# Exponentials handed to ScalarE's DMA queue, and three written-out orders, in a kernel of 64 graphs with two layers of graph attention

## The chip, the cores and the metric

The kernel runs on one core of a Trainium2 chip, in float32. The metric is the device time of one execution in microseconds (us). A core has TensorE (PE; its weight loads are PEld), VectorE (DVE), ScalarE (ACT), GpSimd (POOL) and SyncE (SP); engines run their own instruction streams in order and wait for one another by semaphores. DMAs are issued by an engine's queue and carried out by 16 DMA engines.

## The reference, cut to what matters

There are 64 graphs of 256 nodes with 512 features. Each passes through two layers; the first holds two attention stages (four heads of 256, then one head of 512), the second one stage (eight heads of 64). Weights are shared by all graphs.

```python
def gat_layer(x, mask, W, a_src, a_dst, bias, concat):
    xl = (x @ W).reshape(B, N, H, F)
    e = leaky_relu(asrc[:, :, None, :] + adst[:, None, :, :], 0.2)   # asrc, adst: xl . a_src, xl . a_dst
    attn = softmax(where(mask[..., None], e, NEG_INF), axis=1)
    out = einsum('bsdh,bshf->bdhf', attn, xl)
    return out + bias
# layer 0
h = maximum(layernorm(x), 0)
mask = (adj > 0) | eye(N)
x = x + gat_layer(elu(gat_layer(h, mask, W1, ...)), mask, W2, ...)
# layer 1
h = maximum(layernorm(x), 0)
xp = h @ W_proj                              # 8 heads of 64
scores = leaky_relu(a_src_i + a_dst_j + b_att, 0.2), -1e30 where adj is 0
x = x + relu(softmax(scores, axis=-1) @ xp)
```

## The kernel before

A graph is taken as two tiles of 128 nodes. Each large product (m1a and m1b for the two halves of W1, m2 for W2, m3 for W_proj) is a `Product`: seven smaller products p1 to p7 in place of eight, of sums and differences of operand blocks. Its matmuls are at L54; ACT copies the partial sums that are still needed (`kept`, L60); `put` adds and writes the results (`total`, L251 on ACT, L253 on DVE). TensorE's results go to three pools of PSUM banks: `ps_mm` (4 banks), `ps_sum` (2) and `ps_tr` (2).

The exponential of leaky_relu(a + o) is the larger of two products of exponentials, so only vectors go through the exponential function. `exp1`, `exp2` and `exp3` compute three vectors each on ACT (L275, and L461 to L465 for the third stage), and `spread` lays one of them out along the free axis on all partitions: a small DMA writes it to DRAM (`kept`, L240), further ones read it back as `bc` rows (L245; two heads each). Both are issued by SP. Then `edges1`, `edges2`, `edges3` call `weigh` once per tile: ACT writes `wy` (L280, three buffers), DVE writes the weights `e` (L281, nine buffers), masked by `mask` (L299, L301) or by `cap`, which `caps` makes on ACT (L308 to L312) and `cap3` transposes by two DMAs of SP (L363).

The steps of a graph are, in order of data: `load` (SP), `stats1` and `norm1` (L170 to L178, ACT's L195), `away1` (two DMAs of SP through DRAM that rearrange blocks of 32 for the transpose, L207 and L208), `turn1` (DVE's 32 x 32 transposes L213, then POOL's sums L219 to L222; graph 0 has `turn0`, L342 and L343, in their place), m1a and m1b, `exp1`, `edges1`, `gat1` (L382), `out1` (DVE L390 and L392, then ACT's two `ez`, L395 and L396), `elu1` (L401), `turn2` (TensorE L201, ACT L410), m2, `exp2`, `edges2`, `gat2` (L433), `out2` (L440, L443), `stats3`, `norm3`, `turn3` (L201, L233), m3, `exp3`, `edges3`, `gat3` (L482), `out3` (L488, L490, POOL's L492), `range` (L495, L496; the ranges of the exponentials), and `store` (SP, L499, 512 KB from `x2`). POOL's `bias` (L352) adds the second stage's bias to the input. A second, general program follows the loop; it starts only if a range is extreme.

For `norm1` ACT writes its output in a mixed order of columns, so that the block that DVE's L213 reads after the two DMAs is contiguous.

The program text sets each engine's order. One string, `order`, lists the steps of a round with an offset for the graph; the loop over r from -1 to 66 runs it for each round and leaves out steps of graphs that don't exist. So up to four graphs are in work at once, and the first and last graphs follow the same order with holes in it. The products of graph 0's m1b and its 32 dots (`dot`, DVE: attention vectors folded into W1's columns) are written ahead of the loop; further dots for W2, W_proj's products and sums (POOL's L593, DVE's L595) and the differences of weight blocks (`right`, L518), come from two generators, one piece after each step.

Of the kernel before, what the change touches and what calls it, by code (L numbers as in the profile page):

```python
# [17 lines left out]
P = 128  # L18
# [79 lines left out]
def short_path(ctx, tc, flags, x, adj, w1, att_src1, att_dst1, b1, w2, att_src2, att_dst2, b2, w_proj, w_att,  # L98
# [84 lines left out]


    def mixed(h):
        return h.rearrange("p (a c i) -> p a c i", a=4, c=4)

    def unmixed(x):
        return x.rearrange("p (a i c) -> p a c i", a=4, c=4)

    def norm(src, rstd, off, mix):
        h = work.tile([P, T, D], F32, name="h", bufs=1)
        for t in range(T):
            to, of = (mixed(h[:, t]), unmixed(src[:, t])) if mix else (h[:, t, :], src[:, t, :])
            nc.scalar.activation(to, of, AF.Relu, bias=off[:, t:t + 1], scale=rstd[:, t:t + 1])  # L195
        return h
# [6 lines left out]
    def away(h):  # L203


        kept = dram.tile([T, 4, P, P], F32, name="kept_h")
        nc.sync.dma_start(kept.rearrange("t a p e -> p t a e"), h.rearrange("p t (a e) -> p t a e", a=4))  # L207
        nc.sync.dma_start(h, kept.rearrange("t a (j q) e -> (a j) t (q e)", q=4))  # L208

    def back(h, a):  # L210

        for t in range(T):
            nc.vector.transpose(a[:, 4 * t:4 * t + 2].rearrange("p r k (j q) -> p q (r k) j", q=4),  # L213
                                h[:, t].rearrange("p (q c i) -> p q c i", q=4, c=4))
# [22 lines left out]
    def spread(w, heads):  # L237

        kept = dram.tile([heads, P, T], F32, name=f"kept{heads}")
        nc.sync.dma_start(kept.rearrange("h p t -> p h t"), w)  # L240
# [6 lines left out]
        return rows  # L247

# [34 lines left out]
    class Graph:  # L283
# [41 lines left out]
        def norm1(self):  # L325
            self.h = norm(self.xs, *self.ro, True)
# [88 lines left out]
        def exp2(self):  # L415
            exps(lambda sl: self.ex2[:, sl].rearrange("p h t -> p t h"), 1, xl2[:, :, 0, :L2], xl2[:, :, 1, :L2])
            self.bc2 = spread(self.ex2[:, 2:3], 1)

        def edges2(self):
            e = self.e[2] = work.tile([P, T, N], F32, name="e", bufs=9)  # L420
            for s in range(T):
                weigh(e[:, s, :], self.bc2[0], self.ex2[:, 0, s:s + 1], self.ex2[:, 1, s:s + 1],
# [31 lines left out]
        def norm3(self):  # L454
            self.h = norm(self.x2, *self.ro, False)
# [4 lines left out]
        def exp3(self):  # L460
# [6 lines left out]
            self.bc3 = spread(self.ex3[:, 2], H3)  # L467

        def edges3(self, h):
            e = self.e[3, h] = work.tile([P, T, N], F32, name="e", bufs=9)  # L470
            for s in range(T):
                weigh(e[:, s, :], self.bc3[h], self.ex3[:, 0, h, s:s + 1], self.ex3[:, 1, h, s:s + 1],
# [54 lines left out]
    va2 = small.tile([P, HC, 2, 2], F32, name="va2", bufs=1)  # L527
    graphs[0].load()
# [8 lines left out]
    graphs[0].turn0()  # L537
# [10 lines left out]
    def column(r, s, h, c):  # L548
        dot(blocks(w1_sb[0])[r][s][:, c, h:h + 1], blocks(w1_sb[h // 2])[r][h % 2][:, c, -Q:], att1[s][:, h, :])


    dots = [(r, s, h, c) for i in range(2) for s in range(2) for r in range(2) for h in (2 - 2 * i, 3 - 2 * i)
            for c in range(2)]
    first = [d for d in dots if d[0] == 0 and d[2] == 3]
    for d in first:
        dots.remove(d)
        column(*d)
    for _ in right(w1_sb[1]):
        pass
    m1b = graphs[0].m1[1]  # L560
    for part in (m1b.p1, m1b.p2, m1b.p5, m1b.p6, m1b.p7, m1b.c22, m1b.p4, m1b.p3):
        part()
        for d in dots[:4]:
            column(*d)
        del dots[:4]
    for _ in right(w1_sb[0]):
        pass

    def weights_for_0():
        for r in range(2):  # L570
            for c in range(4):
                for s in range(2):
                    for half in range(2):
                        dot(va2[:, 4 * r + c, s, half:half + 1], blocks(w2_sb)[r][half][:, c, -Q:],
                            att2[s][:, half * Q:(half + 1) * Q])
                    yield
        for r in range(2):
            for s in range(2):
                v = va2[:, 4 * r:4 * r + 4, s]
# [331 lines left out]
```

## Time and profile before

| what | value |
|---|---|
| median of 3 runs | 3298.52 us (3297.95 to 3301.16) |
| profiled execution, its own time | 3308.74 us |
| its span, first to last instruction | 3307.0 us |
| mean granted TensorE clock | 0.988 |
| busy share of PE, DVE, ACT, POOL | 95%, 68%, 61%, 35% |
| DMA traffic | 280.36 MB, mean 85 GB/s |

A busy share is the time in which an engine executes, as a share of the span. A group of instructions is one line of the kernel on one engine: its busy time and the mean duration of one, then the idle time of the engine just ahead of them, and what ended most of it. In a timeline the columns are start, duration, engine, line, operation, operands and count; the wait ahead of it stands in brackets, with what ended it. In a row of windows the first figures are the stretch and its length, then busy time (and instructions) of PE, PEld, DVE, ACT and POOL, then the granted clock, the DMA share and GB/s.

### The profile page before, as it was taken

Reading aid. Unit: us, or ns where it says so; the run is one execution under the profiler, and the core shown is the slowest. Engines: PE = TensorE matmul, PEld = TensorE weight load, DVE = VectorE, ACT = ScalarE, POOL = GpSimd, SP = SyncE. Lnnn points to the kernel's source line nnn. Section 1 sums busy time; section 2 is a strip of 40 time slices with the busy share of each in tenths; the row PEclk is TensorE's granted clock in tenths of the full one; section 3 lists DMA queues with packets and bytes.
Section 4 is the critical chain, followed back from the end, with each engine's and each line's share of the span. In section 5 each row is a group of like instructions: output and inputs, shape, how many; then the busy total and the mean of one; then the engine's idle time right before and its main releaser. Section 6 shows DMA issues by size and latency. Waiting matters only on the chain. (4 is left out here: it accounts for less than half of the span.)

```text
span 3307.0 us, 60191 instructions
## 1 busy us (share of the span) xinstructions
PE 3153.8 (95%) x21772; PEld 2657.8 (80%) x21772; DVE 2237.4 (68%) x6189; ACT 2031.4 (61%) x4867; POOL 1172.9 (35%) x1433
## 2 busy tenths in 40 slices
PE   4999999999999999999999999999999999999996
PEld 3788888888888888888888878888888888888885
DVE  7567667667667666676676676676676676766764
ACT  2566666666666666666666665666666666666663
POOL 2343343342332333433433433433423323334332
PEclk7999999999999999999999999999999999999998
DMA  4232332323333333323223333223233333232231
GB/s 132 61 87 78 93 87 78 93 78 87 86 82 90 85 82 90 79 82 92 82 84 93 81 78 93 87 78 91 78 89 86 82 90 85 81 92 81 80 87 48
DMA packets 352653, 280.36 MB, mean 85 GB/s; under 512 B 159200, under 2 KB 253408, under 8 KB 352352
## 3 DMA queue, kind: packets, MB, share of 16 engines
q1 hardware_dynamic: 350976, 274.35, 30.4%
q8 instruction: 176, 2.88, 0.4%
q10 hardware_dynamic: 1376, 2.10, 0.2%
q14 instruction: 125, 1.02, 0.2%
HBM read 200.54 MB, written 67.44 MB: 81 GB/s over the span
## 5 line engine op out<-in xcount | busy, mean ns | idle before, releaser
L280 ACT ACTIVATE wy<-bc,exs 128x256 f32<-128x256 f32 x1664 | 761.7, 524 | 328.6 <-DMA bc<-kept 276.7
L382 PE MATMUL pm<-xl,e 128*128 128x257 f32 x2048 | 504.9, 390 | 95.2 <-DVE e L281 45.0
L253 DVE TENSOR_TENSOR xl<-pm,kept 128x256 f32<-128x256 f32 (+2 forms) x768 | 321.1, 418 | 360.0 <-PE pm L54 285.8
L60 ACT ACTIVATE kept<-sum 128x264 f32<-128x264 f32 (+3 forms) x768 | 286.3, 381 | 399.3 <-PE sum L54 399.2
L281 DVE SCALAR_TENSOR_TENSOR e<-wy,exs,cap 128x256 f32<-128x256 f32 x1024 | 450.8, 481 | 110.2 <-ACT wy L280 110.2
L382 PEld LDWEIGHTS pm<-xl,e 128*128 128x128 f32 x2048 | 356.0, 190 | 207.8 <-DVE e L281 69.2
L54 PE MATMUL sum<-w_sb,h1s 128*128 128x257 f32 x2048 | 489.3, 381 | 2.7 <-ACT h1s L410 1.9
L492 POOL TENSOR_TENSOR x<-x,o 128x256 f32<-128x256 f32 x256 | 196.8, 769 | 788.2 <-DVE o L490 788.2
L54 PEld LDWEIGHTS sum<-w_sb,h1s 128*128 128x128 f32 x2048 | 389.8, 191 | 62.8 <-ACT h1s L410 2.3
L281 DVE SCALAR_TENSOR_TENSOR e<-wy,exs,mask 128x256 f32<-128x256 f32 x640 | 303.2, 527 | 111.1 <-ACT wy L280 111.1
L54 PE MATMUL pm<-w_sb,h1s 128*128 128x257 f32 x1536 | 366.9, 381 | 0.0
L178 POOL TENSOR_TENSOR rstd<-ve,neg_half 128x2 f32<-128x2 f32 x128 | 90.0, 703 | 670.2 <-DVE ve L176 663.8
L54 PEld LDWEIGHTS pm<-w_sb,h1s 128*128 128x128 f32 x1536 | 288.8, 190 | 47.4 <-ACT h1s L410 0.2
L482 PEld LDWEIGHTS pm<-xl,e 128*64 128x64 f32 x8192 | 255.3, 139 | 57.5 <-issue 30.9
L482 PE MATMUL pm<-xl,e 128*64 128x65 f32 x8192 | 274.0, 225 | 13.2 <-DVE e L281 13.0
L54 PE MATMUL sum<-w1a_sb,hs 128*128 128x260 f32 x1024 | 274.1, 390 | 4.5 <-ACT kept L60 1.7
L54 PE MATMUL sum<-wp_sb,hs 128*128 128x264 f32 x1024 | 271.0, 387 | 0.5 <-ACT kept L60 0.5
L54 PE MATMUL sum<-w1b_sb,hs 128*128 128x256 f32 x1024 | 264.0, 380 | 3.0 <-ACT hs L343 1.9
L392 DVE SCALAR_TENSOR_TENSOR z<-pm,r,b_sb 128x256 f32<-128x256 f32 x512 | 247.9, 484 | 18.3
L433 PE MATMUL pm<-xl,e 128*128 128x257 f32 (+1 forms) x1024 | 244.0, 381 | 1.8 <-DVE e L281 1.8
L395 ACT ACTIVATE ez<-z 128x512 f32<-128x512 f32 x256 | 160.1, 626 | 127.0 <-DVE z L392 127.0
L54 PEld LDWEIGHTS sum<-w1a_sb,hs 128*128 128x128 f32 x1024 | 189.7, 191 | 47.1 <-issue 13.7
(94 smaller groups left out, 4998.8 us busy)
## 6 DMA issues: line engine op xcount, KB each, us to landing
bc<-kept SPq DMA_DIRECT2D x384, 256.0 KB, 3.7
xs<-in_x_dram SPq DMA_DIRECT2D x64, 512.0 KB, 3.9
out_dram<-x SPq DMA_DIRECT2D x64, 512.0 KB, 8.5
kept_h<-h SPq DMA_DIRECT2D x63, 512.0 KB, 3.2
h<-kept_h SPq DMA_DIRECT2D x63, 512.0 KB, 3.6
ad<-in_adj_dram SPq DMA_DIRECT2D x64, 256.0 KB, 4.7
bc<-kept SPq DMA_DIRECT2D x64, 128.0 KB, 4.0
w_sb<-in_L_gnn_W_dram SPq DMA_DIRECT2D x4, 512.0 KB
```

The costliest lines, as they stand in the source:

```text
L54: self.nc.tensor.matmul(to[:, :self.n], self.lhs[:, i, c, :], self.rhs[:, i, c, :], start=(first and c == 0), stop=(last and c == self.nk ...
L60: self.nc.scalar.activation(s[:, :self.n], self.sum[:, :self.n], AF.Copy)
L178: nc.gpsimd.tensor_tensor(rstd, ve[:, 0, :], neg_half, ALU.pow)
L253: nc.vector.tensor_tensor(dst, pm, add, ALU.add)
L280: nc.scalar.activation(wy, bc, AF.Copy, scale=yw)
L281: nc.vector.scalar_tensor_tensor(dst, wy.rearrange("p t q -> p (t q)"), xw, mask, ALU.max, op)
L382: nc.tensor.matmul(pm[:, :Q + 1], self.e[1, h][:, s, t * P:(t + 1) * P], xl1[:, s, h, L1:], start=(s == 0), stop=(s == T - 1))
L392: nc.vector.scalar_tensor_tensor(z[:, sl], pm[:, :Q], r, b1_sb[:, sl], ALU.mult, ALU.add)
L395: nc.scalar.activation(ez, z[:, 2 * g * F1:2 * (g + 1) * F1], AF.Relu, scale=-1.0)
L433: nc.tensor.matmul(pm[:, :n], self.e[2][:, s, t * P:(t + 1) * P], xl2[:, s, half, L2:L2 + n], start=(s == 0), stop=(s == T - 1))
L482: nc.tensor.matmul(pv[q:q + 64, h, :], self.e[3, a * G + h][:, s, t * P + q:t * P + q + 64], xl3[:, s, a * G + h, :], start=(s == 0), stop ...
L492: nc.gpsimd.tensor_tensor(to, to, o.rearrange("p h k -> p (h k)"), ALU.add)
```

## The change

The row of exponentials is written from ACT's queue in `spread`. `norm` writes its columns in order for both layers, and DVE's transpose reads with a step of four elements. For the last graph `spread_at_once` makes the rows of stages two and three by matmuls with the identity, into a PSUM bank that ACT reads. The single order becomes three: `head` for the first round, with all weight pieces as steps of their own (class `Weights`), `order` for the rounds between, and `tail` for the end.

```diff
@@ -180,19 +180,11 @@
             nc.gpsimd.tensor_tensor(off, ve[:, 1, :], rstd, ALU.mult)
             return rstd, off
 
-    def mixed(h):
-        return h.rearrange("p (a c i) -> p a c i", a=4, c=4)
-
-    def unmixed(x):
-        return x.rearrange("p (a i c) -> p a c i", a=4, c=4)
-
-    def norm(src, rstd, off, mix):
+    def norm(src, rstd, off):
         h = work.tile([P, T, D], F32, name="h", bufs=1)
         for t in range(T):
-            to, of = (mixed(h[:, t]), unmixed(src[:, t])) if mix else (h[:, t, :], src[:, t, :])
-            nc.scalar.activation(to, of, AF.Relu, bias=off[:, t:t + 1], scale=rstd[:, t:t + 1])
+            nc.scalar.activation(h[:, t, :], src[:, t, :], AF.Relu, bias=off[:, t:t + 1],
+                                 scale=rstd[:, t:t + 1])
         return h
 
     def turn(h, c, pt):
@@ -211,7 +204,7 @@
 
         for t in range(T):
             nc.vector.transpose(a[:, 4 * t:4 * t + 2].rearrange("p r k (j q) -> p q (r k) j", q=4),
-                                h[:, t].rearrange("p (q c i) -> p q c i", q=4, c=4))
+                                h[:, t].rearrange("p (q i c) -> p q c i", q=4, c=4))
 
     def left(a, nk):
 
@@ -237,7 +230,7 @@
     def spread(w, heads):
 
         kept = dram.tile([heads, P, T], F32, name=f"kept{heads}")
-        nc.sync.dma_start(kept.rearrange("h p t -> p h t"), w)
+        nc.scalar.dma_start(kept.rearrange("h p t -> p h t"), w)
         rows = []
         for h in range(0, heads, 2):
             k = min(2, heads)
@@ -245,6 +238,13 @@
             nc.sync.dma_start(bc.rearrange("p h q t -> p (h q t)"), rows_of(kept[h:h + k], k * N))
             rows += [bc[:, i].rearrange("p q t -> p t q") for i in range(k)]
         return rows
+
+    def spread_at_once(w, heads, h):
+
+        pm = ps_mm.tile([P, 512], F32, name="pm")
+        for t in range(T):
+            nc.tensor.matmul(pm[:, t * P:(t + 1) * P], w[:, h, t:t + 1].to_broadcast([P, P]), ident, start=True, stop=True)
+        return pm[:, :N].rearrange("p (t q) -> p t q", t=T)
 
     def total(dst, pm, add):
         if add is None:
@@ -323,7 +323,7 @@
             self.ex3 = exs[:, 6 * (H1 + 1):].rearrange("p (i h t) -> p i h t", i=3, t=T)
 
         def norm1(self):
-            self.h = norm(self.xs, *self.ro, True)
+            self.h = norm(self.xs, *self.ro)
 
 
         def norm0(self):
@@ -414,12 +414,13 @@
 
         def exp2(self):
             exps(lambda sl: self.ex2[:, sl].rearrange("p h t -> p t h"), 1, xl2[:, :, 0, :L2], xl2[:, :, 1, :L2])
-            self.bc2 = spread(self.ex2[:, 2:3], 1)
+            self.bc2 = None if self.b == B - 1 else spread(self.ex2[:, 2:3], 1)
 
         def edges2(self):
             e = self.e[2] = work.tile([P, T, N], F32, name="e", bufs=9)
+            bc = self.bc2[0] if self.bc2 else spread_at_once(self.ex2[:, 2:3], 1, 0)
             for s in range(T):
-                weigh(e[:, s, :], self.bc2[0], self.ex2[:, 0, s:s + 1], self.ex2[:, 1, s:s + 1],
+                weigh(e[:, s, :], bc, self.ex2[:, 0, s:s + 1], self.ex2[:, 1, s:s + 1],
                       self.mask[:, s, :], ALU.mult)
 
         def gat2(self, t):
...
@@ -464,12 +465,13 @@
             for i, at, by in ((2, G, SLOPE - 1.0), (0, 0, 1.0), (1, 0, SLOPE)):
                 nc.scalar.activation(self.ex3[:, i].rearrange("p (a h) t -> p t a h", a=2), lg3[:, :, :, at:at + G],
                                      AF.Exp, scale=by)
-            self.bc3 = spread(self.ex3[:, 2], H3)
+            self.bc3 = None if self.b == B - 1 else spread(self.ex3[:, 2], H3)
 
         def edges3(self, h):
             e = self.e[3, h] = work.tile([P, T, N], F32, name="e", bufs=9)
+            bc = self.bc3[h] if self.bc3 else spread_at_once(self.ex3[:, 2], H3, h)
             for s in range(T):
-                weigh(e[:, s, :], self.bc3[h], self.ex3[:, 0, h, s:s + 1], self.ex3[:, 1, h, s:s + 1],
+                weigh(e[:, s, :], bc, self.ex3[:, 0, h, s:s + 1], self.ex3[:, 1, h, s:s + 1],
                       self.cap[:, s, :], ALU.min)
 
         def gat3(self, a, t):
@@ -534,7 +537,6 @@
     graphs[0].norm0()
...
-    graphs[0].turn0()
...
@@ -545,95 +547,114 @@
-    for d in first:
-        dots.remove(d)
-        column(*d)
-    for _ in right(w1_sb[1]):
-        pass
-    m1b = graphs[0].m1[1]
-    for part in (m1b.p1, m1b.p2, m1b.p5, m1b.p6, m1b.p7, m1b.c22, m1b.p4, m1b.p3):
-        part()
-        for d in dots[:4]:
-            column(*d)
-        del dots[:4]
-    for _ in right(w1_sb[0]):
-        pass
-
...
+    class Weights:
+        def __init__(self):
+            self.dots = sorted(((r, s, h, c) for s in range(2) for r in range(2) for h in range(H1) for c in range(2)),
+                               key=lambda d: (d[2] < 2, d[0] > 0 or d[2] % 2 == 0, d[1]))
+            self.sums = {}
+        def dots1(self, i):
+            for r, s, h, c in self.dots[4 * i:4 * i + 4]:
+                dot(blocks(w1_sb[0])[r][s][:, c, h:h + 1], blocks(w1_sb[h // 2])[r][h % 2][:, c, -Q:], att1[s][:, h, :])
+        def sums1(self, i):
+            for _ in right(w1_sb[i]):
+                pass
+        def dots2(self, i):
...
+        def columns2(self):
...
+        def sums2(self, i):
+            next(self.sums[2])
+        def load3(self):
...
+        def dots3(self, i):
...
+        def sums3(self, i):
+            if i == 0:
+                self.sums[3] = right(wp_sb)
+            next(self.sums[3])
+    head = """
+        0 turn0, w dots1 0, 0 masks, 0 m1b p1, w dots1 2, w dots1 5, w sums1 1, w dots1 1, 0 m1b p6, w dots1
+        3, 0 bias, 0 m1b p2, 0 m1b p7, w dots2 0, 0 m1b p5, w dots1 4, w dots1 6, w dots1 7, 0 m1a p1, w
+        sums1 0, 0 m1b c22, 0 m1b p4, 0 m1a p6, w dots2 3, 0 m1a p7, 0 m1a p5, w dots2 2, w dots2 7, w dots2
+        5, 0 m1a p2, 0 m1a c22, w dots2 1, 0 m1a p3, w dots2 6, 0 m1a p4, w dots2 4, w columns2, 0 m1b p3, w
+        sums2 0, w sums2 1, 0 exp1, w sums2 2, 0 caps, w sums2 3, 0 edges1 1, 0 edges1 0, 0 edges1 3, 0
+        cap3, 0 edges1 2, 0 gat1 0 0, 0 out1 0 0, 0 gat1 0 1, 0 out1 0 1, 0 gat1 1 0, 0 elu1 0 0, 0 out1 1
+        0, 0 elu1 0 1, w load3, 0 gat1 1 1, 1 load, 0 out1 1 1, w dots3 7, 1 stats1, 0 turn2 0 0, 0 elu1 1
+        0, 1 masks, 0 turn2 0 1, 0 elu1 1 1, 1 norm1, w dots3 1, 0 m2 p1, w dots3 2, w dots3 0, w dots3 6, 1
+        away1, 0 turn2 1 0, 0 turn2 1 1, w dots3 5, w dots3 4, w dots3 3, 1 turn1, 0 m2 p6, w sums3 0, 0 m2
+        p2, w sums3 1, w sums3 2, 0 m2 p7, 0 m2 p4, 0 m2 p5, 1 m1a p1, 1 m1a p6, 0 m2 c22, 1 m1a p5, 0 m2
+        p3, 0 exp2, 1 m1a p7, 1 m1a c22, 1 m1b p1, w sums3 3, 1 m1a p4, 1 m1a p3, 1 m1a p2, 1 exp1, 1 bias,
+        1 m1b p6, 1 m1b p2, 1 m1b p5, 1 caps
+    """
     order = """
-        0 m1a c22, -3 store, -2 edges3 2, 0 m1a p2, -2 edges3 4, 0 m1a p3, -2 edges3 3, 0 m1a p4, 0 exp1, -2
-        edges3 6, 0 m1b p2, -2 edges3 5, 0 m1b p6, -2 gat3 0 1, -2 gat3 0 0, 0 m1b p5, -2 out3 0 1, -1
-        edges2, -2 edges3 7, -2 out3 0 0, 0 m1b p7, -1 gat2 0, 0 m1b c22, -1 out2 0, -1 stats3 0, 0 m1b p3,
-        0 cap3, 0 edges1 0, -1 gat2 1, 0 edges1 1, -1 out2 1, 0 edges1 3, 0 m1b p4, 0 gat1 0 0, 0 edges1 2,
-        1 load, -2 gat3 1 0, 0 out1 0 0, -2 gat3 1 1, 0 gat1 0 1, -1 stats3 1, -1 norm3, -2 out3 1 0, -2
-        range, 0 out1 0 1, 0 gat1 1 0, -1 turn3, 0 elu1 0 0, -2 out3 1 1, 0 gat1 1 1, 0 out1 1 0, 0 elu1 0
-        1, -1 m3 p1, 0 out1 1 1, 1 stats1, -1 m3 p2, 0 elu1 1 1, 0 elu1 1 0, 1 masks, -1 m3 p6, 0 turn2 0 0,
-        0 turn2 0 1, -1 m3 p5, 1 norm1, 0 m2 p1, 0 turn2 1 0, 1 away1, 0 turn2 1 1, -1 m3 p7, -1 m3 c22, 0
-        m2 p2, -1 m3 p4, -1 m3 p3, -1 exp3, 0 m2 p6, 0 m2 p5, 1 bias, 1 turn1, 0 m2 p7, 1 m1a p1, 0 m2 p4, 0
-        m2 c22, 1 caps, 0 m2 p3, 0 exp2, 1 m1a p6, -1 edges3 0, -1 edges3 1, 1 m1b p1, 1 m1a p7, 1 m1a p5
+        -2 edges3 7, -2 gat3 0 0, -2 edges3 5, -2 gat3 0 1, -1 edges2, 0 m1b p7, -2 out3 0 1, -2 out3 0 0,
+        -1 gat2 0, 0 m1b c22, -1 out2 0, -1 stats3 0, 0 m1b p3, -1 gat2 1, 0 edges1 0, 0 edges1 1, 0 m1b p4,
+        -1 out2 1, 0 cap3, 1 load, 0 gat1 0 0, 0 edges1 2, 0 edges1 3, 0 out1 0 0, -2 gat3 1 1, -2 gat3 1 0,
+        -1 stats3 1, 0 gat1 0 1, -1 norm3, -2 out3 1 1, -2 out3 1 0, 0 out1 0 1, 0 elu1 0 0, 0 elu1 0 1, 0
+        gat1 1 0, -1 turn3, 0 out1 1 0, 0 gat1 1 1, 0 out1 1 1, 1 stats1, -1 m3 p1, 0 turn2 0 0, 0 turn2 0
+        1, 0 elu1 1 1, 0 elu1 1 0, -1 m3 p2, -1 m3 p5, 1 masks, 1 norm1, -1 m3 p6, 0 m2 p1, 0 turn2 1 0, 0
+        turn2 1 1, 1 away1, -1 m3 p7, 1 bias, -1 m3 c22, 0 m2 p2, -1 m3 p4, -2 range, -1 m3 p3, -1 exp3, 1
+        turn1, 0 m2 p6, 0 m2 p5, 0 m2 p7, 1 caps, 1 m1a p1, 0 m2 c22, 0 m2 p3, 0 m2 p4, 0 exp2, 1 m1a p6, -2
+        store, -1 edges3 0, -1 edges3 1, 1 m1b p1, 1 m1a p7, 1 m1a p5, 1 m1a c22, -1 edges3 2, 1 m1a p2, -1
+        edges3 4, 1 m1a p3, -1 edges3 3, 1 m1a p4, 1 m1b p2, 1 exp1, -1 edges3 6, 1 m1b p6, 1 m1b p5
     """
-    done = {"load", "stats1", "norm1", "away1", "turn1", "m1b"}
-    pieces = {"turn2": weights_for_0(), "turn3": weights_for_1()}
-    for r in range(-1, B + 3):
-        for off, what, *args in (item.split() for item in order.split(",")):
-            b = r + int(off)
-            if not 0 <= b < B or b == 0 and what in done:
-                continue
-            for name in list(pieces):
-                if what == name:
-                    for _ in pieces.pop(name):
-                        pass
-            of = graphs[b]
-            if what in ("m1a", "m1b"):
+    tail = """
+        -2 range, 0 m1b p5, 0 m1a p2, -1 edges2, -2 gat3 0 0, 0 m1a c22, 0 m1b p6, -2 gat3 0 1, -2 out3 0 1,
+        0 m1b p2, -2 edges3 5, -1 gat2 0, 0 exp1, 0 m1a p4, -1 out2 0, -1 stats3 0, -2 edges3 7, -1 gat2 1,
+        -2 gat3 1 0, -1 out2 1, -1 stats3 1, -1 norm3, -2 out3 0 0, -2 gat3 1 1, -2 out3 1 1, -1 turn3, -1
+        m3 p1, -1 m3 p2, -1 m3 p5, -1 m3 p6, -1 m3 p7, -1 m3 c22, -2 out3 1 0, -1 m3 p4, -1 m3 p3, -1 exp3,
+        -1 range, -1 edges3 1, -1 edges3 4, -1 edges3 0, -1 edges3 3, -1 edges3 2, -1 edges3 5, -1 edges3 7,
+        -1 edges3 6, -1 gat3 0 0, -1 gat3 0 1, -2 store, -1 gat3 1 1, -1 out3 0 1, -1 out3 1 1, -1 gat3 1 0,
+        -1 out3 0 0, -1 out3 1 0, -1 store
+    """
+    weights = Weights()
+
+    def run(steps, r):
+        for at, what, *args in (item.split() for item in steps.split(",")):
+            if at == "w":
+                of = weights
+            else:
+                of = graphs[r + int(at)] if 0 <= r + int(at) < B else None
+            if of and what in ("m1a", "m1b"):
                 of = of.m1["ab".index(what[2])]
                 what = args.pop(0)
-            elif what in ("m2", "m3"):
+            elif of and what in ("m2", "m3"):
                 of = getattr(of, what)
                 what = args.pop(0)
-            getattr(of, what)(*map(int, args))
-            for name in list(pieces):
-                if next(pieces[name], pieces) is pieces:
-                    del pieces[name]
-                else:
-                    break
+            if of:
+                getattr(of, what)(*map(int, args))
+
+    run(head, 0)
+    for r in range(1, B):
+        run(order, r)
+    run(tail, B)
 
     top = small.tile([P, 4], F32, name="top")
     nc.vector.tensor_reduce(top[:, 0:1], ends[:, 0, :], AX.X, ALU.max)
```

## The prediction, made before the changed kernel ran

> **What bounds the kernel now.** I read the shares by engine first, then the windows, then the groups of instructions (what ended TensorE's idle time), then one round of the timeline.
>
> ```profile
> PE 3153.8 (95%) x21772; PEld 2657.8 (80%) x21772; DVE 2237.4 (68%) x6189; ACT 2031.4 (61%) x4867; POOL 1172.9 (35%) x1433
> 0.00:100.00 100.00, 57.42 (x190) 43.03 (x191) 68.20 (x225) 28.60 (x61) 33.36 (x45) 0.80 0.36 115
> 100.00:160.00 60.00, 56.58 (x313) 46.95 (x312) 37.17 (x97) 33.83 (x84) 16.67 (x20) 0.97 0.30 71
> 160.00:3230.00 3070.00, 2988.43 (x20861) 2525.77 (x20860) 2099.54 (x5775) 1941.39 (x4654) 1104.93 (x1346) 1.00 0.31 85
> 3230.00:3301.00 71.00, 51.32 (x414) 42.04 (x412) 32.40 (x94) 27.57 (x69) 17.91 (x23) 0.81 0.18 47
> ...
> L382 PE MATMUL pm<-xl,e 128*128 128x257 f32 x2048 | 504.9, 390 | 95.2 <-DVE e L281 45.0 <-DVE r L390 34.6 <-DVE o L490 15.6
> ```
>
> TensorE bounds it, and no matmul is removed. So the change can only take TensorE's idle time: 3070 - 2988 = 82 us in the steady part, 46 in the first 160 us, 20 in the last 71. The steady idle time has one place: gat1 (L382) owns 95.2 us, about 14 of it in the first graphs. Graph 1's gat1 starts at 111.35 and graph 63's at 3218.98, so a round is 50.1 us and loses 82/61 = 1.33. Here is one round:
>
> ```profile
> 1001.29 0.32 SPq L245 DMA_DIRECT2D bc<-kept  x1
> 1001.71 1.75 SPq L499 DMA_DIRECT2D out_dram<-x  x1
> ...
> 1003.65 0.45 ACT L275 ACTIVATE exs<-xl 128x8 f32<-128x8 f32 x3
> 1003.88 1.66 SPq L240 DMA_DIRECT2D kept<-exs  x1
> ...
> 1009.92 0.81 SPq L245 DMA_DIRECT2D bc<-kept  x2
> ...
> 1013.51 2.60 ACT L280 ACTIVATE wy<-bc,exs 128x256 f32<-128x256 f32 x6 [4.09 <-DMA bc<-kept]
> 1014.08 1.73 DVE L281 SCALAR_TENSOR_TENSOR e<-wy,exs,mask 128x256 f32<-128x256 f32 x4 [1.55 <-ACT wy L280]
> 1014.61 2.00 PE L382 MATMUL pm<-xl,e 128*128 128x257 f32 x8 [0.43 <-DVE e L281]
> ...
> 1019.12 1.97 PE L382 MATMUL pm<-xl,e 128*128 128x257 f32 x8 [0.48 <-DVE r L390]
> ...
> 1021.35 1.98 PE L382 MATMUL pm<-xl,e 128*128 128x257 f32 x8 [0.26 <-DVE o L490]
> ```
>
> The exponentials end at 1004.10; their 4 KB write has landed at 1009.92, 5.8 us later, because it stands in SP's queue behind the 512 KB store of 1001.71. Then the bc loads, ACT's first wy, DVE's e, and gat1 waits 0.43. The later waits (0.48, 0.26) are the same lateness handed on: DVE starts its eight e's 1.55 us late, so out1 and out3 free gat1's banks late. Before any store runs, the same steps go faster:
>
> ```profile
> 153.03 0.45 ACT L275 ACTIVATE exs<-xl 128x8 f32<-128x8 f32 x3
> 153.26 0.37 SPq L240 DMA_DIRECT2D kept<-exs  x1
> ...
> 156.64 0.79 SPq L245 DMA_DIRECT2D bc<-kept  x2
> ```
>
> Write to load: 156.64 - 153.48 = 3.2 us, and wy starts at 160.69, 7.2 after the exponentials instead of 9.4.
>
> **Edit 1: kept from ACT's queue.** The row gives 5.8 us behind the store and 3.2 without it. The Trainium skill, "DMA: Bandwidth & Descriptors", "Issuing engines are not separate DMA queues", speaks against the edit: DMAs of all engines share the same 16 DMA engines, and another issuer saves only the sequencer's time. Read so, the landing stays at 5.8 and the round at 50.1. But the same page ("Queues, rings and completion order") says that SP and ACT own one ring each and that a DMA engine alternates between rings by packets; then the small write doesn't wait for 512 KB. No row here has both rings busy with such a write. Ends: 3.2 and 5.8; I take 4, nearer the uncontended row. Then bc is issued about 1008.2 and wy could start near 1011.7, but DVE is in other work to 1012.5, so e starts there. gat1's e is ready by about 1013.0 against TensorE's 1014.2: wait gone, 1 us spare. out1's first z then ends 1.5 us earlier, near 1017.5, and out3's o near 1019.8, with the range reductions (0.36) moved later as well; TensorE wants the banks at about 1018.2 and 1020.1, so the margins are 0.7 and 0.3. All three waits fall: -81. After a wait the group also restarts slowly (504.9 busy for 2048 against gat2's 244.0 for 1024, 17 us over); I count 12.
>
> What it adds: three issues per round on ACT, in order. An issue costs 0.32 to 0.38 on SP and, before, 0.37 to 0.66 on ACT in the first 15 us; I take 0.37, plus 0.1 to 0.2 in which ACT waits for its own last exponential. From 1045.6 to 1053 and 1000.1 to 1006.1 ACT has no pause over 0.35 us, so this pushes everything queued behind: wy of edges3 6, 7, 5, then of edges2, whose e gat2 needs. The new order pays most of exp2's part: caps (L308 to L312, 2.2 us of ACT from 1045.59) is moved up behind the sum of 1042.70, into ACT's pauses of 0.49 and 1.35 before 1045.31, and p4 now comes after p3. exp1's part, 0.6, remains, and edges3 7 (two wy, 0.85) now precedes edges2. My replay: edges2's wy 1007.5 to 1008.4, e at 1008.6 and 1009.0, against gat2 at 1008.83 and 1009.07: zero to 0.2 us late. I charge 0.15 x 61 = +9. SP loses three waits for exponentials, so nothing on it moves later; the store still precedes exp1's loads.
>
> **Edit 2: plain norm, strided transpose.** Layer 1's L195 takes 1331 ns with the mixed order and 809 without: ACT frees 2 x 0.52 us per round, 0.5 us of it ahead of the transfer's issue at 1032.84. L213 takes 1105 ns each with contiguous input; its new input steps 16 bytes. The trace has no strided DVE read. From below 0 (it is already 2.2 ns per element), from above ACT's own stride price, +0.52. "Advanced Engine Details and Errata", "SBUF Cachelines", asks for two hits per 16-byte line or a penalty, which would just move ACT's 1.04 us to DVE. I take +0.3 each. Cover: DVE idles 2.88 us before L213, and m1a p1 (1042.50) needs only the first transpose, which ended 0.45 before; the earlier norm adds over 1. Without that cover it would cost up to 0.5 x 61 = 32.
>
> **Edit 3: the order within a round.** turn2 goes ahead of m3 p2, norm1 ahead of m3 p6, m2 p3 ahead of p4. I looked at each TensorE step against its operand in this order: m3 p6 needs m3 p1's kept, now behind two ez (0.4 us to spare); m2 p6 needs POOL's second sum (0.7); edges3 0 needs bc3 (1.1). elu1 0 1 stops DVE about 0.9 us for its ez; behind it stands out1 1 0, whose banks m3 p2 wants 2 us later. Of the moved steps' DMAs, cap3's two transposes (2.46 us of SP) go from ahead of edges1 to behind out2 1, followed only by the next graph's load, whose rows DVE wants at 1026.72 and which landed about four us after 1016.82; the store stays between exp2's and exp1's loads; bias (2.36 of POOL) stays between the sums of h1s and hs. All lie beside TensorE's work: cost 0; if one came late, 0.5 us of it per round would be 31.
>
> **Edit 4: head.** The 64 dots (0.35 each) and twelve weight differences stay; they bound it, DVE being busy 68 of 100 us. Before, exp1 comes at 44.1, the eight first e's between 52.22 and 57.75, and reductions of the third weight (L595, waiting for POOL's L593) and L518 stand between the elus until 80.2, with m2's first sum at 74.12 and its last product at 94.33. New: caps (ACT kept m1a's p7 waiting 1.69 at 36.18) comes after exp1, and m1a's p6 to p4, six products of about 1.05 cold from 31.8, end at 38.4; put and exponentials, 39.3. But DVE has w2's sums to about 51, so gat1 starts at 51.5, little earlier; the elus then end near 68 and m2 near 88. TensorE gains about 8 us: -8 (0 to -14).
>
> **Edit 5: the last graph.** From exp3's last exponential (3281.57) to the first wy (3289.01) 7.4 us pass in two DMAs. Two matmuls instead (0.28 each in a warm row, 0.43 in L342's cold one), about 0.7: -6.7. exp2's round trip (wy at 3259.74 after 3252.1) is hidden under fourteen wy except 1.75: -1.7; ranges off the end and a warmer gat2, -1.6. ACT then reads PSUM, as in L410, at no more. Sum -10 (-6 to -13).
>
> **Sum.** -81 - 12 + 9 - 8 - 10 = -102. The profiled run took 3308.74 (span 3307.0), 10.2 above the median 3298.52. 3298.5 - 102 = 3196.5, and I round toward the small margins: 3200.
>
> **Rivals.**
> - A new wait takes half (0.22): jitter or a dearer issue makes edges2 or a product 0.7 us late per round. For: ACT's row of wy without pause. Against: edges2's bc2 costs ACT 0.40 before and should come earlier. +34 on 3200: about 3235 to 3250.
> - The write doesn't get past the store, as the rule says (0.09): gat1's waits stay, head and tail remain: 3298.5 - 18 - 5 = 3275. For: landings in one queue go up to 6.7. Against: the packets of the two rings need not queue.
> - Slower (0.05): ACT is held by the issue. SP's L240 took 1.66 at 1003.88, the maximum over 192. If exp1's issue held ACT 2.6 us every round, edges2's e would be 2.6 - 0.37 - 0.15 = 2.1 late for gat2, 0.5 more than the 1.5 gained: 61 x 0.5 - 18 = +13, 3312. It decides from about 2.3 us. Against: medians of 0.36.
> - No effect within 0.2% (0.02; that is what a measurement here tells from nothing): the first two at once.
>
> The main case has 0.62, its own range 3175 to 3225. With the second it holds 0.84, less its far ends: 3175 to 3255. Faster 0.93, same 0.02, slower 0.05.
>
> **What would show it.** After: kept's landing near 4 us on ACT's queue in rounds with a store; gat1's idle time under 20 us; in the steady window TensorE busy over 98.5%; a new small wait, if any, at gat2 for DVE e. L213 between 1105 and 1630 ns. First wy under 1 us after the last exp3. Wrong would be: gat1 still waiting for e, or ACT's issues over 1 us, or an idle TensorE at m1a p1 behind L213.

## The result, and the profile after

The changed kernel takes 3270.94 us (median of four runs, 3269.88 to 3281.43) against 3298.27 for the kernel before on the same chip: ratio 0.9922, 95% interval 0.9901 to 0.9943. The forecast was 3200, with a range of 3175 to 3255. The direction was right; the gain was 27 us where 98 were forecast, and the time lies outside the range.

The profiled execution took 3281.43 us with a span of 3279.7, which is 27.3 under the span of before. First the engine shares of its page, then the same stretches as before; the steady one ends about ten us behind the start of the last graph's gat1, as before.

```profile
PE 3155.8 (96%) x21808; PEld 2663.1 (81%) x21808; DVE 2267.6 (69%) x6189; ACT 1959.6 (60%) x4867; POOL 1178.3 (36%) x1433
```

The windows (the figures after the length are busy times of PE, PEld, DVE, ACT and POOL, granted clock, DMA share and GB/s):

```profile
0.00:100.00 100.00, 57.89 (x213) 44.93 (x214) 69.81 (x228) 27.70 (x64) 33.23 (x44) 0.86 0.38 116
100.00:160.00 60.00, 55.92 (x331) 46.33 (x331) 40.74 (x107) 36.44 (x90) 17.05 (x21) 1.00 0.31 74
160.00:3209.00 3049.00, 2987.29 (x20823) 2527.57 (x20819) 2123.90 (x5755) 1867.93 (x4644) 1110.72 (x1346) 1.00 0.31 85
3209.00:3279.70 70.70, 54.68 (x453) 44.30 (x451) 33.15 (x102) 27.51 (x70) 17.33 (x22) 0.88 0.12 39
```

In the steady stretch TensorE is still idle for 3049 - 2987 = 62 us, where the forecast left almost nothing of 82. The groups of the page say where (busy time and mean, then the idle time ahead of them):

```profile
L382 PE MATMUL pm<-xl,e 128*128 128x257 f32 x2048 | 500.3, 387 | 57.5 <-DVE e L281 21.7
...
L54 PE MATMUL pm<-w_sb,h1s 128*128 128x257 f32 x1536 | 370.7, 383 | 10.4 <-DVE xl L253 7.1
```

gat1 (L382) kept 57.5 of its 95.2 us, and m2 (the second line) has a new wait of 10.4 us; it had none before. One round of the timeline shows why gat1 still waits; it is to be laid beside the round shown of before:

```profile
988.51 1.07 SPq L501 DMA_DIRECT2D out_dram<-x  x1
991.20 0.37 ACTq L233 DMA_DIRECT2D kept<-exs  x1
996.39 0.79 SPq L238 DMA_DIRECT2D bc<-kept  x2
...
999.97 1.79 ACT L280 ACTIVATE wy<-bc,exs 128x256 f32<-128x256 f32 x4 [3.23 <-DMA bc<-kept]
1000.53 1.74 DVE L281 SCALAR_TENSOR_TENSOR e<-wy,exs,mask 128x256 f32<-128x256 f32 x4 [0.71 <-ACT wy L280]
...
1001.34 1.90 PE L382 MATMUL pm<-xl,e 128*128 128x257 f32 x8
...
1005.59 1.97 PE L382 MATMUL pm<-xl,e 128*128 128x257 f32 x8 [0.34 <-DVE r L390]
...
1007.81 1.97 PE L382 MATMUL pm<-xl,e 128*128 128x257 f32 x8 [0.25 <-DVE r L490]
```

ACT issues the write of the exponentials at 991.20, in 0.37 us, and SP may load the rows only at 996.39. The write is on another queue than the store of 988.51 and still takes 5.2 us. This round has no wait for e at gat1, but the two waits for PSUM banks are as before, since DVE starts its eight e's late (0.71 idle, waiting for wy) and so comes late to out1 and out3.

By place, from the traces: graph 3's gat1 starts at 206.57 instead of 212.23 (head: -5.7 us); from there to graph 63's gat1 it takes 2992.0 instead of 3006.8 (sixty rounds: -14.7); from there to the end 81.1 instead of 88.0 (tail: -6.9). The sum is -27.3.

For the experiments one more figure is used throughout: the landing of exp1's kept, from its issue to the first load of its rows, as a median over the rounds of the trace. It is 6.2 us before and 5.8 after. (By "landing" is meant the moment from which what the DMA wrote may be used; where a trace records it, the loads follow it within 0.1 us.)

### The profile page after: what moved, and what is told of

Read it like the earlier page. It is cut to its first block, busy times and chain, and to the rows that moved or that the text cites. A ratio compares the mean times of both kernels' runs of the same rounds, so it can differ in the third digit from the quotient of the medians.

```text
span 3279.7 us, 60652 instructions
## 1 busy us (share of the span) xinstructions
PE 3155.8 (96%) x21808; PEld 2663.1 (81%) x21808; DVE 2267.6 (69%) x6189; ACT 1959.6 (60%) x4867; POOL 1178.3 (36%) x1433
## 3 DMA queue, kind: packets, MB, share of 16 engines
q14 instruction: 126, 1.03, 0.2%
## 5 line engine op out<-in xcount | busy, mean ns | idle before, releaser
L280 ACT ACTIVATE wy<-bc,exs 128x256 f32<-128x256 f32 x1646 | 746.9, 524 | 263.8 <-DMA bc<-kept 199.4
L382 PE MATMUL pm<-xl,e 128*128 128x257 f32 x2048 | 500.3, 387 | 57.5 <-DVE e L281 21.7
L494 POOL TENSOR_TENSOR x<-x,o 128x256 f32<-128x256 f32 x256 | 181.0, 728 | 930.9 <-DVE r L490 884.2
L382 PEld LDWEIGHTS pm<-xl,e 128*128 128x128 f32 x2048 | 365.5, 190 | 151.4 <-DVE e L281 36.5
L60 ACT ACTIVATE kept<-sum 128x264 f32<-128x264 f32 (+3 forms) x768 | 276.7, 376 | 310.7 <-PE sum L54 294.3
L54 PE MATMUL pm<-w_sb,h1s 128*128 128x257 f32 x1536 | 370.7, 383 | 10.4 <-DVE xl L253 7.1
L178 POOL TENSOR_TENSOR rstd<-ve,neg_half 128x2 f32<-128x2 f32 x128 | 117.6, 919 | 683.5 <-DVE ve L176 683.5
L281 DVE SCALAR_TENSOR_TENSOR e<-wy,exs,mask 128x256 f32<-128x256 f32 x640 | 276.0, 482 | 65.9 <-ACT wy L280 65.6
L54 PE MATMUL sum<-w1b_sb,hs 128*128 128x256 f32 x1024 | 271.7, 388 | 4.1 <-ACT hs L343 1.9
```

What stands on the lines that cost most here:

```text
L54: self.nc.tensor.matmul(to[:, :self.n], self.lhs[:, i, c, :], self.rhs[:, i, c, :], start=(first and c == 0), stop=(last and c == self.nk ...
L60: self.nc.scalar.activation(s[:, :self.n], self.sum[:, :self.n], AF.Copy)
L178: nc.gpsimd.tensor_tensor(rstd, ve[:, 0, :], neg_half, ALU.pow)
L280: nc.scalar.activation(wy, bc, AF.Copy, scale=yw)
L281: nc.vector.scalar_tensor_tensor(dst, wy.rearrange("p t q -> p (t q)"), xw, mask, ALU.max, op)
L382: nc.tensor.matmul(pm[:, :Q + 1], self.e[1, h][:, s, t * P:(t + 1) * P], xl1[:, s, h, L1:], start=(s == 0), stop=(s == T - 1))
```

## The experiments

They ran on three other chips than the result: e1 to e4 on chip 1, "after, again" and e5 to e7 on chip 2, e8 to e11 on chip 3. There the kernel before takes 3277, 3281 and 3283 us, so all comparisons are ratios to the kernel before, measured in the same series. Expectations in us of e1 to e4 were worked out from the result's chip and are read as shares of its 3298. "Idle" is TensorE's idle time in one round, as a mean of 56 rounds (graphs 4 to 60) of the trace. Traces differ between chips too: the two rows of the changed kernel have landings of 5.8 and 5.3 us and idle times of 1.03 and 0.75. The kernel before has a trace from the result's chip alone.

| kernel | chip | store | kept by | ratio to before (interval) | landing us | round us | idle us |
|---|---|---|---|---|---|---|---|
| before | result | late | SP | 1 | 6.2 | 50.12 | 1.35 |
| after | result | late | ACT | 0.9922 | 5.8 | 49.88 | 1.03 |
| after, again | 2 | late | ACT | 0.9932 (0.9917 to 0.9947) | 5.3 | 49.51 | 0.75 |
| e2: after | 1 | late | SP | 0.9948 (0.9934 to 0.9962) | 4.6 | 49.45 | 0.69 |
| e5: before | 2 | late | ACT | 0.9985 (0.9978 to 0.9992) | 5.5 | 49.70 | 0.83 |
| e1: after | 1 | early | ACT | 0.9808 (0.9795 to 0.9821) | 3.9 | 48.84 | 0.23 |
| e8: after | 3 | early | SP | 0.9842 (0.9828 to 0.9856) | 3.8 | 49.06 | 0.41 |
| e3: before | 1 | early | SP | 0.9742 (0.9728 to 0.9755) | 3.7 | 48.25 | 0.02 |
| e7: old order, new head and tail | 2 | early | SP | 0.9703 (0.9689 to 0.9716) | 3.8 | 48.29 | 0.04 |
| e10: e7 | 3 | early | ACT | 0.9816 (0.9802 to 0.9829) | 3.7 | 48.90 | 0.20 |

Two theories stood at the start. Theory S: the small write lands late because the 512 KB of the store are still being written, whichever queue issued it. Theory R: ACT's own queue did free it, and what is left is the write's own time.

**e1: the changed kernel, store moved.**

```diff
-... 0 exp2, 1 m1a p6, -2 store, -1 edges3 0, ...
+... 1 stats1, -2 store, -1 m3 p1, ...
```

> The changed kernel with one step moved within the round: the store of graph -2 from ahead of edges3 0 (where SP issues it 2.7 us ahead of exp1's kept) to behind stats1, some 28 us earlier, when its rows have just been finished by POOL. Theory S (the small write lands late because the 512 KB of the store are still being written, whichever queue issued it): kept of exp1 lands 3.1 us after its issue instead of 5.8, gat1's wait for e (0.22 us a round) goes, its waits for out1 and out3 (0.35 and 0.22) shrink to about half, since DVE has 0.7 us idle ahead of the first e and no more: round 49.9 to about 49.3, 3225 to 3246 us. Theory R (ACT's own queue already freed the write from the store, and what is left of the landing is its own time): landing stays at 5.5 to 5.8, time 3268 to 3274.

Measured: 3215.35 us, 0.9808 of before. Landing falls to 3.9. One round, and the group of gat1 in the whole trace of e1:

```profile
977.08 0.37 ACTq L233 DMA_DIRECT2D kept<-exs  x1
...
981.25 0.81 SPq L238 DMA_DIRECT2D bc<-kept  x2
...
984.88 1.78 ACT L280 ACTIVATE wy<-bc,exs 128x256 f32<-128x256 f32 x4 [2.27 <-DMA bc<-kept]
985.61 1.66 DVE L281 SCALAR_TENSOR_TENSOR e<-wy,exs,mask 128x256 f32<-128x256 f32 x4
987.22 1.90 PE L382 MATMUL pm<-xl,e 128*128 128x257 f32 x8
...
L382 PE MATMUL pm<-xl,e 128*128 128x257 f32 x2048 | 494.3, 387 | 10.5 <-DVE e L281 9.0 <-DVE r L390 0.9 <-DVE r L490 0.5
```

Of its 10.5 us, 8.8 belong to graph 0's first gat1, in the head; all three waits are gone from the rounds, at once (0.01 us a round is left), where theory S had the two bank waits halved. As a share of 3298 its range is 0.978 to 0.984, so the time lies in it; theory R's 0.991 to 0.993 is out. The gain isn't that x2 comes free sooner: in the changed kernel's list of waits (total, times, longest) DVE waits for a store only once.

```profile
DVE x L444 <- DMA out_dram<-x: 0.3, 1, 0.3
```

The store gains as well. These are its own landings, first in the kernel before (7 of 64 recorded), then in e1 (55 of 64):

```profile
DMA to landing us min/median/max: 7.7/8.5/9.2
...
DMA to landing us min/median/max: 2.8/2.8/4.9
```

In its late place SP issues it 0.4 us behind the 128 KB row load of stage two, and its first packet comes 2.4 us after the issue instead of 0.9. So the write stood behind a store that was itself slow; that the row load is the reason is likely, but wasn't tried alone.

**e2: the changed kernel, kept issued by SP.**

```diff
-        nc.scalar.dma_start(kept.rearrange("h p t -> p h t"), w)
+        nc.sync.dma_start(kept.rearrange("h p t -> p h t"), w)
```

> The changed kernel with kept issued by SP again; everything else as changed. Theory S (another queue saves only a little, because the store's bytes are in the way of the write in both): kept lands about 0.4 us later than from ACT's queue (6.2 against 5.8), gat1 waits about 0.2 us more a round: 3278 to 3290 us. Theory R (the queue is what the change gained): most of the 20 us that the middle rounds gained is lost, and SP's waits for exponentials come on top: 3290 to 3300.

> The changed kernel once more, on the same chip as the runs beside it, since the kernel before took 3277 us on the chip of the first experiments and 3298 on that of the result. Both theories: 0.990 to 0.994 of the kernel before, that is 3245 to 3258 us if this chip gives 3277. It gives the measure for kept issued by SP in the new order (0.9948 of before): theory S (the queue matters little) expects the two within 0.3%, theory R (the queue is what was gained) the changed kernel at least 0.6% ahead.

Measured: e2 3258.88 us, the changed kernel again 3259.18, ratios 0.9948 and 0.9932. Their intervals overlap: in this order the queue is worth nothing that these runs can tell. e2 lies in theory S's range (0.994 to 0.998 of 3298), and theory R, which wanted 0.6% between the two, falls here. The landing from SP's queue (4.6) is no longer than from ACT's (5.3, but on another chip; e4, from ACT's queue on e2's chip, has 5.1). One round of e2:

```profile
980.08 0.39 SPq L501 DMA_DIRECT2D out_dram<-x  x1
983.21 0.37 SPq L233 DMA_DIRECT2D kept<-exs  x1
988.28 0.81 SPq L238 DMA_DIRECT2D bc<-kept  x2
```

The traces also show what the write lands behind. In all 53 rounds for which one records both landings (7 of before and 38 of e2, with the write on SP's queue, 8 of the changed kernel again, with it on ACT's) the write lands after the store, at the median 0.2 to 0.3 us after it.

**e3: the kernel before, store moved, nothing else.**

```diff
-... 0 m1a c22, -3 store, -2 edges3 2, ...
+... 0 out1 1 1, -2 store, 1 stats1, ...
```

> The kernel before with one step moved: the store from ahead of edges3 2 of the next round to ahead of stats1, some 40 us earlier; kept stays on SP's queue. Theory S: kept of exp1 lands after 3.2 us instead of 6.2, e starts up to 1.5 us earlier, gat1's waits fall from 1.35 us a round to under 0.5: 3240 to 3268 us, so more than the whole change. Theory R (it needs the other queue): landing falls by at most 1 us and the time stays above 3285.

Measured: 3194.07 us, 0.9742 of before. One step moved in the old order brings over three times what the whole change brought. Here are the page's shares by engine and gat1's group:

```profile
PE 3121.4 (98%) x21772; PEld 2671.0 (84%) x21772; DVE 2226.2 (70%) x6189; ACT 2035.6 (64%) x4867; POOL 1172.7 (37%) x1433
...
L382 PE MATMUL pm<-xl,e 128*128 128x257 f32 x2048 | 487.7, 385 | 14.8 <-DVE e L281 8.9
```

The waits are at 0.02 us a round (1.35 before, on the result's chip). The expectation's best was 0.982 of 3298, so it was too cautious by some 27 us. TensorE's busy time is lower as well, 3121.4 us against 3153.8 with the same 21772 instructions. Nearly all of that is gat1's: counted from the end of the matmul before, its matmuls take 7.17 us a round against 7.67. That they run denser because e is there in time is likely, but not shown, and part of the difference is the chip's: the two traces differ by 114 us, the ratio stands for 85.

**e11: the changed kernel, store moved by a few steps only.**

```diff
-... 0 m2 p4, 0 exp2, 1 m1a p6, -2 store, ...
+... 0 m2 p4, -2 store, 0 exp2, 1 m1a p6, ...
```

> The changed kernel with the store only a few steps earlier: ahead of exp2 instead of behind it, so that SP issues it some 4 to 6 us sooner; nothing else moved. Theory S (the overlap with the store's bytes delays the write): at exp1's kept most of the store has been written, it lands after 4 us or less; the time goes most of the way to that of the early store (0.9808), 0.982 to 0.987 of before, unless exp2's kept, now in the store's wake, comes too late. Theory E (the early store helps for another reason, such as freeing x2 sooner): nothing gained, 0.991 to 0.995.

Measured: 3257.29 us, 0.9932 of before (0.9917 to 0.9947): nothing gained, against theory S's number, and theory E's number to the letter. The timeline shows what happened:

```profile
980.62 0.39 SPq L501 DMA_DIRECT2D out_dram<-x  x1
983.18 0.34 ACTq L233 DMA_DIRECT2D kept<-exs  x1
989.35 0.37 ACTq L233 DMA_DIRECT2D kept<-exs  x1
990.00 4.18 SPq L238 DMA_DIRECT2D bc<-kept  x3
```

Now exp2's kept (983.18) stands in the store's wake; it lands after 4.8 us (median) instead of 2.9. SP takes its loads in order, so the row load of stage two comes 6.8 us after that write in this round, and its 128 KB are issued beside exp1's kept of 989.35, which lands after 4.6 instead of 5.3. In the 23 rounds with both landings recorded exp2's kept now lands after the store, 0.3 us at the median. gat1's waits fall from 0.54 to 0.31 us a round, and gat2 gets a wait for e (0.07). The delay was handed to the other small write. Theory E, as an explanation, has the row of waits above against it.

**e5: the kernel before, kept issued by ACT.** Edit as e2's, the other way.

> The kernel before with the one edit that kept is issued by ACT; order, norm, head and tail as before. Theory S: landing behind the store falls by 0.4 to 0.6 us only, gat1's waits by as much and ACT pays three issues a round: 0.993 to 1.003 of before. Theory R: landing near 4 us, gat1's wait for e (0.60 a round) gone: 0.98 to 0.99.

Measured: 3277.41 us, 0.9985 (0.9978 to 0.9992): theory S's range, and a gain of 5 us. The landing is 5.5 (6.2 before, but on the result's chip, where the changed kernel too has 0.5 more), and a new wait appears: TensorE waits 0.18 us for ACT's copy L60 at m1a in every one of the 56 rounds.

**e8 and e10: what ACT's issues cost without the store in the way.** e8 is e1 with e2's edit; e10 is e7, described below, with kept issued by ACT.

> The changed kernel with the early store (0.9808 of before) and kept issued by SP, so that ACT issues no DMA. Theory I (three issues of 0.37 us a round on ACT cost TensorE something, charged 9 us in the prediction): the waits for kept (0.06) and xl (0.13) shrink, 0.976 to 0.979 of before. Theory N (they lie in ACT's idle time): within 0.1% of 0.9808.

> The combination (0.9703 of before) with kept issued by ACT. In the old order, with the store in the way, ACT's issues showed as a wait of 0.18 us for kept in every round (11 us in all). Theory I: the same here, 0.973 to 0.974 of before. Theory N: within 0.1% of 0.9703.

In the old order (e10 against e7, 0.9816 against 0.9703) they cost 37 us by the ratios, where theory I had about 11. ACT's stream in e10, at exp2 (columns as in a timeline):

```profile
971.33 0.38 ACT L275 ACTIVATE exs<-xl 128x2 f32<-128x2 f32 x3
971.55 0.34 ACTq L233 DMA_DIRECT2D kept<-exs  x1
971.93 0.39 ACT L60 ACTIVATE kept<-sum 128x260 f32<-128x260 f32 x1 [0.23 <-ACT exs L275]
```

The issue waits for the exponential just ahead of it, and the copy L60 queues behind both; TensorE's next m1a product waits 0.18. That is 0.16 of the 0.61 us a round; the other 0.45 lie in groups of matmuls that take longer, gat1's above all (7.34 us a round against 7.16, counted as above); why they do is not shown. In the new order (e8 against e1) it is the other way: SP's issue costs 11 us by the ratios (0.9842 against 0.9808, the intervals just apart), with waits for L60 (0.06 to 0.13) and for the transpose L206 (0 to 0.12). So each order fits the issuer that it was written for, and theories I and N are both wrong for the new order.

**e4: the changed kernel, norm and transpose as before** (`norm` with its `mix` argument, contiguous input for the transpose).

> The changed kernel with norm and the transpose's input as before (ACT writes norm1's columns in mixed order, DVE reads contiguous blocks). ACT gets 1.05 us a round longer, DVE's transposes 0.03 us shorter each. If norm1 is covered on its way to m1a p1, as the prediction had it: no change, 3268 to 3275. If ACT's time or the later transfer counts (DVE waits for the transfer in 58 rounds, 0.8 us each): up to 0.5 us a round, 3275 to 3302.

Measured: 3312.73 us, 1.0108 of before (1.0092 to 1.0124), some 55 us over the changed kernel, beyond both ranges (at most 1.001 of 3298). The groups of TensorE:

```profile
L54 PE MATMUL sum<-wp_sb,hs 128*128 128x264 f32 x1024 | 274.5, 391 | 48.2 <-ACT kept L60 48.0 <-ACT hs L232 0.3
```

and ACT's stream at that place:

```profile
1032.19 2.52 ACT L193 ACTIVATE h<-xs,off,rstd 128x512 f32<-128x512 f32 x2 [0.76 <-POOL off L180]
...
1034.63 0.64 ACT L60 ACTIVATE kept<-sum 128x264 f32<-128x264 f32 x2
1035.14 1.13 PE L54 MATMUL sum<-wp_sb,hs 128*128 128x264 f32 x4 [0.75 <-ACT kept L60]
```

The new order puts norm1 directly ahead of ACT's copies for m3 p6 and m2 p6. With the mixed norm (2.52 us for two) they come 0.75 us late in every round, which is 46 of the 55 us.

**e6: the kernel before with early store, norm and transpose as changed.**

> The kernel before with the early store, and norm and transpose as changed (plain columns, DVE reads with a step). If the strided read costs DVE nothing that counts and ACT's 1.05 us a round lay beside other work, as the prediction had it: within 0.1% of the kernel with the early store alone (0.9742 of before). If the mixed norm sat on a path in the old order too, as it does in the new order (0.76 us a round at m3 p6): 0.5% to 1% below that; if the strided read pushes DVE's e's: up to 0.5% above.

Measured: 3195.07 us, 0.9737 against e3's 0.9742: no difference. In the old order norm1 had cover, and the strided read costs nothing.

**e7: the combination.** The changed kernel's head, tail, norm and rows by TensorE, around the old order with the early store, kept by SP. Since the old order runs edges3 5 and two gat3 of a graph a few steps sooner, these three items are left out of `tail`.

> The changed kernel's head, tail, plain norm and rows by TensorE, around the old order with the early store; kept issued by SP. If head and tail are worth what the traces of before and after show (5.6 and 6.9 us) and nothing else moves: 12 us under the old order with the early store, 0.970 to 0.971 of before (about 3180 us where before takes 3277). If the head leaves the first rounds of the other order in a worse state, half of it.

Measured: 3183.11 us, 0.9703 of before, the fastest kernel here. It is 11 us under e3, 13 by the ratios, as expected.

**e9: the combination, last graph's rows by DMA.**

> The combination (0.9703 of before: new head and tail, plain norm, old order with the early store, kept by SP) with the last graph's rows written and read by DMA again, as in the kernel before. The prediction gave the rows by TensorE 8.4 us (6.7 for stage three, 1.7 for stage two): 0.9725 to 0.973 of before. If the tail's new order is what gained at the end: within 0.1% of 0.9703.

Measured: 3193.88 us, 0.973 (0.9717 to 0.9744): by the ratios the rows by TensorE are worth 9 us, as expected. By the traces the stretch from graph 63's gat1 to the end is 89.5 us instead of e7's 79.5. From the changed kernel's tail:

```profile
3261.39 0.68 ACT L466 ACTIVATE exs<-lg 128x16 f32<-128x16 f32 x3 [0.70 <-DVE lg L253]
...
3262.47 0.84 ACT L280 ACTIVATE wy<-pm,exs 128x256 f32<-128x256 f32 x2 [0.40 <-PE pm L246]
```

The first wy follows the last exponential by 0.40 us; by DMA it was 7.4.

## Why the prediction was wrong, and where it was right

**The step that failed: "Ends: 3.2 and 5.8; I take 4, nearer the uncontended row."** It measured 5.8 in the result, as a median, where the median before is 6.2 (the 5.8 of the prediction was one round): the upper end. The prediction had the rule that said so, in the Trainium skill's "DMA: Bandwidth & Descriptors", "Issuing engines are not separate DMA queues", and set it aside for the other section of that page, from which it argued that a small write would pass the store between packets. The packets of the write do start among the store's, 0.9 us after the issue where it was 1.2, but e2 has the same 0.9 from SP's own queue, so the second queue is not what does it. And packets are not what the row loads wait for: the last comes after 2.5 us (2.9 before, 2.1 in e2, 1.3 in e1, with the store out of the way), and from there to the landing another 3.1 pass (2.3 in e1). The landing comes just behind the store's own, whichever queue issued the write. That 4 us was possible was a guess; no row had both rings busy with such a write, as the prediction says itself, and the value should have stayed near the row that had the store in it.

**How much hung on it.** In e1 the write lands after 3.9 us, as forecast, and the changed kernel comes to 0.9808 instead of 0.9922 to 0.9932: 38 to 41 us of the 71 that were missing. Most of the rest is the next two steps, edit 3 and the issues on ACT.

**The -81 for gat1's waits.** All of it hung on that landing. Measured in the result's traces: gat1's waits fell by 0.54 us a round, 33 over 61 rounds, and new waits at m2 and m1a took 13 of that back, so TensorE's idle time went from 1.35 to 1.03. That the three waits are one lateness handed on was right: e1 and e3 move the store alone, and all three go together. The size was near, too: in e3 waits and restarts together are worth 0.0258 of before, 85 us, against 93.

**The -12 for slow restarts** can't be told from the waits. In e3 the rest of a round beside the idle time is 48.24 us against 48.77, 32 us over 61 rounds. But with 81 for the idle time that makes 113, and by the ratio e3 gained 85 in all: the two traces are of two chips, on which the kernel before itself takes 3277 and 3298. In the changed kernel the rest of a round didn't fall (48.86).

**The +9 for ACT's issues** was wrong in its basis. An issue took 0.37 as forecast, and edges2 is not where it hurts (gat2 waits for e 1.2 us in all). In the old order the cost is 37 us, 10 of them in waits for the copy L60 of m1a, which the replay did not look at, and the others in longer matmuls. In the new order, ACT is the cheaper issuer by 11 us, so "SP loses three waits for exponentials, so nothing on it moves later" was half the story: SP's waits for exponentials cost something there.

**Edit 3 at 0** is the second step that failed. With the store early, and head, norm and tail alike but for three steps, four runs part the order from the issuer:

| | kept by SP | kept by ACT |
|---|---|---|
| old order | 0.9703 (e7) | 0.9816 (e10) |
| new order | 0.9842 (e8) | 0.9808 (e1) |

Going from e7 to e1, new order and ACT's issues together, costs 34 us where 0 and 9 were charged. With kept by SP the order alone costs 46; with kept by ACT, nothing.

**Edit 2 at 0.** It was right for the old order (e6), where the transpose paid even less than was taken: 1137 ns against 1105, so the +0.3 us did not come. The cover was named at the wrong consumer: m1a p1 was looked at, and the queue behind norm1 on ACT, the copies L60, was not. In the new order it is worth about 55 us, so it is what makes that order possible rather than an extra.

**Head and tail.** The head gave 5.7 of 8; the tail 6.9 of 10. In the first 100 us the granted clock was 0.86 instead of 0.80; how much of the head's gain is the clock's was not separated. The rows by TensorE gave 9 to 10 in e9 against the 8.4 forecast. The rest of the tail's order gave some back: with rows by DMA the stretch from graph 63's gat1 to the end is 89.5 us with the new tail (e9) and 87.7 with the old (e6). Of the list of what would show it, these held: L213's successor between 1105 and 1630 ns, ACT's issues far under 1 us, the first wy under 1 us after exp3. "kept's landing near 4", "gat1's idle time under 20" and "over 98.5%" (2987.29 of 3049 is 98.0%) did not, and the new small wait came at m2 and not at gat2.

**The rival that came true** had 0.09: "The write doesn't get past the store": 3275 forecast, 3270.94 measured. That it is so near is part luck: it had 18 us for head and tail and 5 for the rest, and they gave 12.6 and 14.7. Its mechanism is what e2 and the landings show. The rows to prefer it were there: the rule had an argument against the edit, and no row of the trace supported the other side.

What stays open: which steps of the new order cost TensorE. Beside e3 the trace of e1 shows 0.15 us a round of waits at m2, most of them for xl, and 0.07 at m1a, most for L60, and 0.36 in longer matmuls of m2 and gat1; single steps were not tried. Why matmuls of gat1 take longer in some orders stays open too.

## What to carry to other kernels

When a small transfer on the critical path is late beside a large one, ask when the large one must run, not who issues the small one: moving the store to a quiet stretch, as soon as its rows were done, was worth over three times the whole change. Read the landing, not the packets: here the small write's packets were through long before it could be used. Look for every consumer in the wake, as a store that is moved a little only finds the next small write. A DMA issued by a compute engine takes that engine's place in the line: name the instruction behind it, and who waits for that.

## What the runs showed of the hardware that was not expected

- A write of 1 KB in 128 packets is held up by a 512 KB store about as long as one of 4 KB in 512 packets: exp2's kept lands after 4.8 us instead of 2.9 (e11), exp1's after 5.3 instead of 3.9 (the changed kernel again, and e1).
- Behind the store the small write landed no sooner from a second queue: on one chip 4.6 us from SP's own (e2) and 5.1 from ACT's (e4, which differs in its norm). In all 53 rounds with both landings recorded it landed after the store, by 0.2 to 0.3 us at the median.
- The 512 KB store itself landed after 8.5 us when issued 0.4 us behind a 128 KB row load (before), and after 2.8 in a quiet stretch (e1).
- DVE's transpose with a step of 16 bytes took 1137 ns against 1105, a price of 0.03 us where the prediction took 0.3.
- ACT's wy took 470 ns in the last graph, reading PSUM, against 522 reading SBUF, both in the trace of after (medians).
- The kernel before took 3298 us on one chip and 3277 to 3283 on three others, the changed one 3271 and 3259 on two: 0.4% to 0.6% between chips, so a difference of that size is read only within one series.
